# Five sets of edits in a four-layer cross-attention and RWKV kernel: the order of the first attention, its copies, and where the last norm and the channel mixes keep their data

## The chip, the cores and the metric

The kernel runs on one core of a Trainium2 chip, in one launch. The metric is the device time of that launch in microseconds (us). Three runs of the kernel before gave 2950.38, 2953.61 and 2958.53 us; the median, 2953.61 us, is the time that the change is held against.

The engines are named as in the profile: PE does matrix products and transposes, PEld loads its weights, DVE is the vector engine, ACT the scalar engine, POOL the general one (GpSimd), and SP issues the DMAs. Each engine works through its own instructions in order and waits on semaphores for what others produce.

## The reference, cut to what is computed

There are 8 sequences of 112 tokens and 512 channels (x), and for each a context of 375 rows of 512. Everything is float32. Four layers follow one another:

```python
# layer 0: one-head cross-attention of x on the context
q, k, v = x @ w_q.T, ctx @ w_k.T, ctx @ w_v.T
x = x + alpha * (softmax(q @ k.T / sqrt(512)) @ v) @ w_o.T
# layers 1 and 2: RWKV; the state comes from the first 18 rows of the context
xa = ln(x); sx = shift(xa) - xa                      # time mix
k, w, v, r, g = projections of xa + sx * (maa + lora(xa, sx))
s = k v^T + exp(-exp(w)) * s, token after token      # a scan over 112 tokens
x = x + (group_norm(r s) * silu(g)) @ Wo.T
xc = ln(x)                                           # channel mix
x = x + sigmoid(xr2 @ Wfr.T) * (relu(xk2 @ Wfk.T) ** 2 @ Wfv.T)
# layer 3: two cross-attentions of 16 heads of 128 on the context, then an MLP
x = x + attention(ln1(x), ctx);  x = x + attention(ln2(x), ctx)
x = x + gelu(ln_mlp(x) @ w_fc1 + b_fc1) @ w_fc2 + b_fc2
```

## The kernel before

**Layout.** Channels lie on the 128 partitions in four blocks (NC = 4), tokens along the free axis (896, in two halves of 448). x stays in SBUF from start to end. A pool `wpool` of four 8 KB slots (tag "w") holds the weights of all layers in turn. Each stage opens its own pools and closes them, and the next stage's pools take the same addresses: a pool that overlies a closed one can be used only once that one is free.

**Who orders the instructions.** The code is a Python program that emits instructions; a planner then orders each engine's instructions by their place in the program and by when it expects their inputs. Inside `tc.manual_schedule(engines=ORDERED)` PE, DVE, ACT and POOL keep the written order. In the kernel before only the scan of the time mixes does that (L682). The DMAs of SP are ordered by the planner everywhere.

**Layer 0** (L224 to L356). `w_qk` is formed as a product of the turned (transposed) w_q and w_k, q as its product with x, and `w_vo` from the turned w_v and w_o. Then the loop at L324 goes over the eight sequences: load the next context (four buffers, L232), turn the context into rows (L328, 12 transposes, three PSUM evictions by DVE), four score products (L336), softmax over DVE and ACT (L214 to L220), three transposes of the probabilities (L340), 12 products with the rows (L346), and a copy to z by ACT (L349). The last step, `ps_o`, multiplies z by w_vo; DVE adds it to x (L353). All of layer 0 is left to the planner.

For every second sequence `park` (L251) writes seven combinations of a pair of contexts to DRAM (`blocks`), which later layers read: six plain copies by DVE (L261), eight differences by POOL (L263), and five DMAs (14 for the first pair). It has one SBUF buffer, `blocks`, so a `park` begins when the DMAs of the one before have read it.

**Filling.** `values()` (L823) computes the values and part of the keys of layer 3 from the parked blocks (PE line L933). It is a generator; layers 1 and 2 call `fill(n)` at the places where PE would otherwise wait. It begins by loading weights (L842), four sums of them by POOL (L849 to L852), and a difference of two biases by DVE (L979), which SP then stores (L981).

**Layers 1 and 2.** `rwkv_layers` (L796) builds four constant matrices (`heads`, `same`, an identity; L803 to L816) and runs `rwkv` twice: `time_mix_inputs` (L378; its first steps load W_g, W_v, W_k and W_r and reorder the columns of W_g and W_v by ACT and DVE, L419 and L420), the scan, and `channel_mix` (L723). The channel mix keeps xc, sx, kk, rr, xk2 and xr2 in one pool; rr and kk are used until its last product, the other four only until `ps_fr`.

**The end of layer 2** (L788 to L794). While PE does the second half of `ps_fv`, the first half of layer 3's first norm is computed whole: mean, difference, squares, variance, root, reciprocal (L195), product (L196). `layer_norm_half` (L166) is the helper of all norms; `fills` says how many filler pieces go in at its three PE waits.

**Layer 3.** `attention(1)` (L1199) starts with scale and offset of that first half, the norm of the second half, `token_sums`, and then the first queries (`ps_k1q`, L1093). Beside it `first_keys` (L1239) is the filler: it loads a key weight, sums of it by POOL (L1067 to L1070), contexts and blocks (`cx`, `cs`, `cy`; L1221, L1226, L1228), and gives 28 pieces of four matmul records each (L1166). Its pools are opened in the order near, t3v (`cs`, `wsk`), t3k (`kt`, `cy`), t3, t3w.

Of the kernel before, what the change touches and what calls it, by code (L numbers as in the profile page):

```python
# [22 lines left out]
F32 = mybir.dt.float32  # L23
# [85 lines left out]
def tile_kernel(ctx: ExitStack, tc: tile.TileContext, d: dict, out: bass.AP):  # L109
# [26 lines left out]

    mean_c = const.tile([P, P], F32, name="mean_c")
# [28 lines left out]
    def layer_norm_half(ps, work, y, h, scale, offset, name, room=None, bank=None, fills=(2, 2, 4), small_tag="rstd"):  # L166
# [22 lines left out]
        nc.scalar.activation(sq, y, AF.Square)  # L189
        fill(fills[1])  # L190
        var = over_channels(sq, "var")
        fill(fills[2])
        rstd = small("rstd", "")
        nc.scalar.activation(rstd, var, AF.Sqrt, bias=eps)
        nc.vector.reciprocal(rstd, rstd)  # L195
        nc.vector.tensor_mul(y, y, rstd.unsqueeze(1).to_broadcast([P, NC, NH]))  # L196
        if scale is not None:
            scale_by_channel(y, y, scale, offset)
# [23 lines left out]


    def layer0():  # L224
# [3 lines left out]
        with (  # L228

            tc.tile_pool(name="a0s", bufs=2, space=PSUM) as ps2,  # L230
            tc.tile_pool(name="a0c", bufs=4) as near,
            tc.tile_pool(name="a0", bufs=1) as keep,  # L232
# [18 lines left out]
            def park(b, c1, c2):  # L251
# [7 lines left out]
                for k in range(2):  # L259
                    for y, z in ((b11, c11), (b21, c21), (b22, c22)):  # L260
                        nc.vector.tensor_copy(y[:, k], z[:, k])  # L261
                    for y, z, less in ((t0, c12, c11), (t1, c22, t0), (t2, c22, c12), (t3, c21, t1)):
                        nc.gpsimd.tensor_sub(y[:, k], z[:, k], less[:, k])  # L263
# [22 lines left out]
            def turned(w, name):  # L286

                t = keep.tile([P, NC, C], F32, tag="turned", bufs=3, name=f"t_{name}")
                for o in range(NC):
                    p = mm(ps, f"ps_t{name}_{o}")  # L290
                    for k in range(NC):
                        nc.tensor.transpose(p[:, k * P : (k + 1) * P], w[:, k, o * P : (o + 1) * P], ident)
                    (nc.vector.tensor_copy if o % 2 else nc.scalar.copy)(t[:, o, :], p)
                return t

            def product(a, b, name, pool, scale=1.0):

                y = pool.tile([P, NC, C], F32, tag=name, name=name)
# [9 lines left out]
            w_qk = product(turned(w_q, "q"), turned(w_k, "k"), "w_qk", keep, 1.0 / math.sqrt(C))  # L308
            q = keep.tile([P, NC, N], F32, name="q0")
            z = last.tile([P, NC, N], F32, name="z0")  # L310
            project(
                ps,
                w_qk,
                lambda k, h: halves(x[:, k, :], h),
                lambda o, h, p: nc.scalar.copy(halves(q[:, o, :], h), p),
                "q0",
            )
            w_vo = product(turned(w_v, "v"), w_o, "w_vo", last)
            for b in range(B):
                tok = slice(b * L, (b + 1) * L)  # L320
                if b + 1 < B:
                    context(b + 1)
                cx = cxs[b]
                if b % 2:  # L324
                    park(b, cxs.pop(b - 1), cxs.pop(b))
                rows = work.tile([CT, 3, C], F32, tag="rows", name=f"rows0_{b}")
                for t in range(3):
                    p = mm(ps, f"ps_r0_{b}_{t}")[:CT, :]  # L328
                    for k in range(NC):
                        nc.tensor.transpose(  # L330
                            p[:, k * P : (k + 1) * P], cx[:, k, t * CT : (t + 1) * CT], ident
                        )
                    nc.vector.tensor_copy(rows[:, t, :], p)
                sc = ps2.tile([L, S], F32, tag="sc", name=f"sc0_{b}")
                for k in range(NC):
                    nc.tensor.matmul(sc, q[:, k, tok], cx[:, k, :], start=k == 0, stop=k == NC - 1)  # L336
                prob = softmax(work, sc, S, f"0_{b}")
                pt = ps2.tile([CT, 3, L], F32, tag="pt", name=f"pt0_{b}")
                for t in range(3):
                    nc.tensor.transpose(pt[:, t, :], prob[:, t * CT : (t + 1) * CT], ident[:L, :L])  # L340
                pts = work.tile([CT, 3, L], F32, tag="pts", name=f"pts0_{b}")
                nc.vector.tensor_copy(pts, pt)
                av = ps2.tile([P, NC, L], F32, tag="av", name=f"av0_{b}")
                for o in range(NC):
                    for t in range(3):
                        nc.tensor.matmul(  # L346
                            av[:, o, :], rows[:, t, o * P : (o + 1) * P], pts[:, t, :], start=t == 0, stop=t == 2
                        )
                nc.scalar.copy(z[:, :, tok], av)  # L349
# [33 lines left out]
    def time_mix_inputs(n, pre, names, ones_t, first, k, v, r, g, decay, rows):  # L383
# [7 lines left out]
        with (  # L391
# [21 lines left out]
            ws = {f: weight(f"{pre}W{f}") for f in "gvkr"}  # L413
# [309 lines left out]
    def channel_mix(n, pre, names, first):  # L723
        nonlocal filler
        with (
            tc.tile_pool(name=f"c{n}", bufs=1) as one,
            tc.tile_pool(name=f"cw{n}", bufs=2) as work,
            tc.tile_pool(name=f"cp{n}", bufs=6, space=PSUM) as ps,
        ):
            f_k, f_r, f_v = (weight(pre + names[f]) for f in ("Fk", "Fr", "Fv"))  # L730
# [20 lines left out]
            kk = one.tile([P, NC, N], F32, name=f"kk{n}")  # L751
            rr = one.tile([P, NC, N], F32, name=f"rr{n}")
# [29 lines left out]
            else:  # L782
# [8 lines left out]
                layer_norm_half(ps, work, y, 0, None, None, "ln3_1", ([sq], None), None, (1, 1, 1))  # L791
# [4 lines left out]
    def rwkv_layers():  # L796
        with tc.tile_pool(name="rc", bufs=1) as one:
            ones_t = one.tile([P, P], F32, name="ones_t")
            mean_h = one.tile([P, P], F32, name="mean_h")
            less_mean_h = one.tile([P, P], F32, name="less_mean_h")  # L800
            center_h = less_mean_h, mean_h
            pick = one.tile([P, 4, 4 * HB], F32, name="pick")
            with tc.tile_pool(name="rs", bufs=1) as setup:  # L803
                heads = setup.tile([P, P + P + HS - 1], F32, name="heads")
                nc.sync.dma_start(heads, d["heads"])

                nc.vector.tensor_copy(ones_t.rearrange("p (q h r) -> p q h r", q=4, h=HB), turned(heads[:, :P]))
                same = setup.tile([P, P], F32, name="same")
                for q in range(4):
                    nc.sync.dma_start(same[32 * q : 32 * (q + 1)], turned_rows(d["heads"][:, :P], q))  # L810
                nc.scalar.mul(mean_h.rearrange("p (q h r) -> p q h r", q=4, h=HB), turned(same), 1.0 / HS)
                nc.vector.tensor_sub(less_mean_h, identity(setup, "rs"), mean_h)

                for r in range(4):
                    at = P + HS - 1 - 4 * r
                    nc.vector.tensor_copy(pick[:, r], heads[:, at : at + 16 * HB - 3 : 4])  # L816
            first = one.tile([P, 2, NC, B], F32, name="first")
            nc.sync.dma_start(first, d["first"])
            for n in (1, 2):
                rwkv(n, ones_t, center_h, pick, first)  # L820


    def values():  # L823
# [151 lines left out]
        for i in (1, 2):  # L975
# [3 lines left out]
            nc.vector.tensor_sub(over, over, bv)  # L979
# [219 lines left out]
    def attention(i, ident, h_in, work, kv, ps, ps2, keep, near, mlp_norm):  # L1199
# [61 lines left out]
        for h in range(2):  # L1261
            if i == 1 and not h:
                scale_by_channel(halves(h_in, 0), shared.pop("normed"), *scales)
            else:
                fill(2)
                layer_norm_half(ps, work, halves(h_in, h), h, *scales, f"ln3_{i}", room, ln_bank, (3, 3, 4))
# [276 lines left out]
```

## Time and profile before

| | us |
|---|---|
| median of the runs | 2953.61 |
| the profiled execution | 2960.41 |
| its span, first to last instruction | 2958.3 |
| around the span | 2.1 |
| PE busy | 2862.2 (97%) |
| DVE busy | 1603.7 (54%) |
| ACT busy | 1009.1 (34%) |
| POOL busy | 872.6 (29%) |
| mean granted clock of PE | 0.990 |

The page gives busy time per engine, a strip of 40 slices of the span, the chain of work that ended last, and the costliest groups of instructions. A matmul in float32 appears as two records. A row of the timeline reads: start, duration, engine, line, operation, output and inputs, count. A row of the waits reads: engine, output, line, then whom it waited for, the total in us, how often, the longest. A row of the chain of waits reads: start, duration, what held the end at that time. In a table of windows each engine has its busy time; PEclk is the granted clock as a share of full speed.

By stage, from the windows: layer 0 runs to 162.4 us, the first time mix's inputs to about 350, layer 1's channel mix ends near 780, layer 2's near 1425, and layer 3 takes the rest.

### The profile page before, as it was taken

Reading aid. Unit: us, or ns where it says so; the run is one execution under the profiler, and the core shown is the slowest. Engines: PE = TensorE matmul, PEld = TensorE weight load, DVE = VectorE, ACT = ScalarE, POOL = GpSimd, SP = SyncE. Lnnn points to the kernel's source line nnn. Section 1 sums busy time; section 2 is a strip of 40 time slices with the busy share of each in tenths; the row PEclk is TensorE's granted clock in tenths of the full one; section 3 lists DMA queues with packets and bytes.
Section 4 is the critical chain, followed back from the end, with each engine's and each line's share of the span. In section 5 each row is a group of like instructions: output and inputs, shape, how many; then the busy total and the mean of one; then the engine's idle time right before and its main releaser. Section 6 shows DMA issues by size and latency. Waiting matters only on the chain.

```text
span 2958.3 us, 29826 instructions
## 1 busy us (share of the span) xinstructions
PE 2862.2 (97%) x10130; PEld 1561.7 (53%) x10130; DVE 1603.7 (54%) x2350; ACT 1009.1 (34%) x2004; POOL 872.6 (29%) x700
## 2 busy tenths in 40 slices
PE   8989999999999999999899999999999999999999
PEld 4734443344444433356465656666565656656544
DVE  1564188856342788643455555545555554545455
ACT  2123466534243565532332323232331323323311
POOL 2332178744331687642411010100302010000030
PEclk9999999999999999999999999999999999999999
DMA  6521498943321989642344444334332433432110
GB/s 256 174 70 42 134 284 249 273 129 124 94 67 58 269 239 288 195 137 70 116 130 128 130 128 130 108 119 141 94 120 98 142 108 120 140 112 80 44 53 25
DMA packets 198743, 400.82 MB, mean 135 GB/s; under 512 B 33224, under 2 KB 119528, under 8 KB 191808
## 3 DMA queue, kind: packets, MB, share of 16 engines
q1 hardware_dynamic: 198592, 398.91, 43.3%
q8 instruction: 81, 1.33, 0.2%
q14 instruction: 70, 0.57, 0.1%
HBM read 321.06 MB, written 77.91 MB: 135 GB/s over the span
## 4 chain that ended last, share of the span: by engine, by line
PE 80%; DVE 7%; POOL 4%; DMA 3%; issue 3%; ACT 3%; SPq 0%; DVEq 0%; POOLq 0%; ACTq 0%
PE ps_vk L933 13%; PE ps_k1k L1166 10%; PE ps_k5k L1166 7%; PE av L1335 6%; PE sc L1322 5%; PE pt L1325 3%; PE ps_o L161 3%; PE ps_fk L161 2%; PE ps_k1q L1093 2%; PE ps_r L487 2%; PE ps_k L487 2%; PE ps_k7q L1093 2%; PE ps_fr L161 2%; PE ps_k5q L1093 2%; PE ps_k5o L1093 1%
## 5 line engine op out<-in xcount | busy, mean ns | idle before, releaser
L933 PE MATMUL ps_vk<-wv,cv 128*128 128x512 f32 x1296 | 583.7, 601 | 13.9 <-ACT k L1031 6.3
L933 PEld LDWEIGHTS ps_vk<-wv,cv 128*128 128x128 f32 x1296 | 244.0, 192 | 338.1 <-issue 287.9
L959 POOL TENSOR_TENSOR k<-k,k 128x512 f32<-128x512 f32 (+1 forms) x153 | 200.2, 1309 | 321.5 <-ACT k L958 264.3
L694 DVE TENSOR_TENSOR_SCAN st<-decay,kv 128x904 f32<-128x904 f32 x128 | 260.7, 2037 | 17.9 <-POOL rs L698 4.4
L698 POOL TENSOR_TENSOR rs<-st,r 128x896 f32<-128x896 f32 x128 | 247.0, 1929 | 53.3 <-DVE st L694 44.1
L218 ACT ACTIVATE prob<-sc,top 112x376 f32<-112x376 f32 (+1 forms) x264 | 151.8, 575 | 322.3 <-DVE top L215 194.8
L1322 PE MATMUL sc<-k,q 128*112 128x376 f32 x512 | 201.1, 485 | 0.7 <-ACT prob L218 0.7
L1335 PEld LDWEIGHTS av<-pts,v 125*128 125x128 f32 (+1 forms) x1536 | 185.0, 193 | 31.4 <-DVE pts L1331 16.6
L1315 POOL COPY k<-over_k 128x4 f32<-128x4 f32 x64 | 13.7, 223 | 605.0 <-PE sc L1322 577.0
L1335 PE MATMUL av<-pts,v 125*128 125x112 f32 (+1 forms) x1536 | 189.1, 277 | 2.1 <-DVE pts L1331 1.9
L1166 PE MATMUL ps_k1k<-cs,wsk 128*128 128x375 f32 x480 | 178.7, 481 | 1.5 <-ACT p1k L1169 1.5
L215 DVE TENSOR_REDUCE top<-sc 112x1 f32<-112x376 f32 (+1 forms) x264 | 143.3, 544 | 64.2 <-PE sc L1322 52.0
L690 DVE TENSOR_TENSOR kv<-vp,k 128x904 f32<-128x904 f32 x128 | 141.4, 1105 | 60.0 <-ACT vp L592 54.6
L958 ACT COPY k<-ps_vk 128x512 f32<-128x512 f32 (+1 forms) x153 | 89.1, 583 | 174.7 <-PE ps_vk L933 172.0
L1031 ACT COPY k<-ps_vk 128x512 f32<-128x512 f32 (+1 forms) x153 | 89.1, 582 | 163.2 <-PE ps_vk L933 156.0
L1325 PEld LDWEIGHTS pt<-ident_l,prob 112*125 112x125 f32 (+1 forms) x768 | 97.9, 177 | 73.2 <-DVE prob L220 44.2
L1325 PE MATMUL pt<-ident_l,prob 112*125 112x112 f32 (+1 forms) x768 | 121.4, 277 | 3.4 <-DVE prob L220 2.3
L220 DVE TENSOR_SCALAR prob<-prob,total 112x376 f32<-112x376 f32 (+1 forms) x264 | 119.7, 454 | 8.0
L1166 PEld LDWEIGHTS ps_k1k<-cs,wsk 128*128 128x128 f32 x480 | 89.7, 190 | 59.8 <-issue 2.1
L592 ACT COPY vp<-vj 128x896 f32<-128x896 f32 x124 | 112.8, 910 | 10.8 <-DMA vj<-rows 6.9
L1173 DVE TENSOR_TENSOR k<-ps_k5k,u2k 128x375 f32<-128x375 f32 x52 | 28.5, 548 | 159.2 <-PE ps_k5k L1166 158.2
L1342 DVE TENSOR_TENSOR ctxt<-av,bv 128x448 f32<-128x448 f32 x64 | 39.9, 624 | 127.3 <-PE av L1335 127.2
(389 smaller groups left out, 4820.6 us busy)
## 6 DMA issues: line engine op xcount, KB each, us to landing
vj<-rows SPq DMA_DIRECT2D x124, 448.0 KB
cv<-blocks SPq DMA_DIRECT2D x181, 251.5 KB
cs<-blocks SPq DMA_DIRECT2D x120, 375.0 KB
wvs<-k SPq DMA_DIRECT2D x128, 256.0 KB
v<-wvs SPq DMA_DIRECT2D x64, 512.0 KB
cx<-in_ctxT SPq DMA_DIRECT2D x38, 750.0 KB
v<-wvs SPq DMA_DIRECT2D x64, 252.0 KB
wvs<-k SPq DMA_DIRECT2D x64, 224.0 KB
```

Of the source, the lines that this page charges most:

```text
L161: nc.tensor.matmul(p, w[:, k, o * P : (o + 1) * P], rhs(k, h), start=k == 0, stop=k == NC - 1)
L215: nc.vector.tensor_reduce(top, scores, AX.X, ALU.max, negate=True)
L218: nc.scalar.activation(prob, scores, AF.Exp, bias=top, accum_out=total)
L694: nc.vector.tensor_tensor_scan(flat(st), flat(decay[:, c]), flat(kv), 0.0, ALU.mult, ALU.add)
L698: nc.gpsimd.tensor_mul(by_batch(rs), st[:, :, :L], by_batch(r[:, c, :]))
L933: nc.tensor.matmul(to, left, right, start=start and n == 0, stop=k == 1, skip_group_check=True)
L959: nc.gpsimd.tensor_add(y, z, y)
L1093: nc.tensor.matmul(to, lhsT, rhs, start=start and k == 0, stop=k == 1, skip_group_check=not start)
L1166: nc.tensor.matmul(y, lhsT, rhs, start=start and k == 0, stop=k == 1, skip_group_check=True)
L1322: nc.tensor.matmul(sc, q[:, o, tok], kt[:, o, :], start=True, stop=True)
L1325: nc.tensor.transpose(pt[t][:nt, o, :], prob[:, t0 : t0 + nt], ident[:L, :L])
L1335: nc.tensor.matmul(av[:, o, :], v[:nt, t, o * HD : (o + 1) * HD], pts[:nt, t, o, :], start=t == 0, stop=t == 2,)
```

## The change

- **Layer 0** is written in an explicit order, in a `manual_schedule`, from the turned weights to the last copy to z. Each turn of the loop does the turning and scores of sequence b+1 and, between them, the transposes of the probabilities of b; the softmax of b+1 is split in two, with the products of b behind it.
- Six context buffers in place of four; contexts 1 to 5 are loaded at once, 6 and 7 in the loop.
- `w_qk` and the turned w_v move into `wpool`.
- The six copies of `park` go from DVE to ACT; the bias difference of `values` goes from DVE to POOL.
- The constant matrices are built in layer 0 (`patterns`), their loads issued behind contexts 1 to 5.
- The RWKV weights are requested in the order k, g, r, v.
- The channel mix has two pools, `lower` and `upper`. In layer 2 xc, sx, xk2 and xr2 are in the lower one and kk and rr in the upper one; in layer 1 the reverse.
- The first half of layer 3's first norm stops after the root (`hold`). Its reciprocal and product are done inside the norm of the second half, and its scale and offset after that.

The core of the diff (the new `patterns` holds what L803 to L816 held):

```diff
-    def layer_norm_half(..., small_tag="rstd"):
+    def layer_norm_half(..., small_tag="rstd", hold=False, beside=iter(())):
         nc.scalar.activation(sq, y, AF.Square)
+        next(beside, None)
         fill(fills[1])
         var = over_channels(sq, "var")
+        next(beside, None)
         fill(fills[2])
-        rstd = small("rstd", "")
+        rstd = sq[:, 0] if hold else small("rstd", "")
         nc.scalar.activation(rstd, var, AF.Sqrt, bias=eps)
-        nc.vector.reciprocal(rstd, rstd)
-        nc.vector.tensor_mul(y, y, rstd...)
-        if scale is not None:
-            scale_by_channel(y, y, scale, offset)
+        def scaled():
+            nc.vector.reciprocal(rstd, rstd)
+            yield
+            nc.vector.tensor_mul(y, y, rstd...)
+            if scale is not None:
+                scale_by_channel(y, y, scale, offset)
+            yield
+        if hold:
+            return scaled()
+        for _ in scaled():
+            pass
...
-            tc.tile_pool(name="a0c", bufs=4) as near,
-            tc.tile_pool(name="a0", bufs=1) as keep,
+            tc.tile_pool(name="a0c", bufs=6) as near,
+            tc.tile_pool(name="a0", bufs=2) as keep,
...
                     for y, z in ((b11, c11), (b21, c21), (b22, c22)):
-                        nc.vector.tensor_copy(y[:, k], z[:, k])
+                        nc.scalar.copy(y[:, k], z[:, k])
...
+            for b in range(1, 6):
+                context(b)
+            made = patterns(keep, ident)
+            next(made)
+            def scores(b, between):
...
+                turn(0)
+                turn(1)
+                part(0)
+                part(1)
+                turn(2)
+                between()
+                part(2)
+                part(3)
+                return rows, sc
...
+            with tc.manual_schedule(engines=ORDERED):
+                w_qk = product(turned(w_q, "q"), turned(w_k, "k"), "w_qk", wpool, "w", 1.0 / math.sqrt(C))
+                project(ps, w_qk, ..., "q0")
+                w_vo = product(turned(w_v, "v", wpool, "w"), w_o, "w_vo", last, "w_vo")
+                next(made)
+                rows, sc = scores(0, lambda: None)
+                park(1, cxs[0], cxs[1])
+                prob = normalized(*exponentials(0, sc))
+                for b in range(B):
+                    if b in (1, 2):
+                        context(b + 5)
...
+                    left = rows
+                    if b + 1 < B:
+                        rows, sc = scores(b + 1, transposes)
+                        prob, total = exponentials(b + 1, sc)
+                    else:
+                        transposes()
+                    if b in (1, 3, 5):
+                        park(b + 2, cxs[b + 1], cxs[b + 2])
+                    if b + 1 < B:
+                        normalized(prob, total)
+                    av = ps2.tile([P, NC, L], F32, tag="av", name=f"av0_{b}")
...
+                    nc.scalar.copy(z[:, :, b * L : (b + 1) * L], av)
...
-            ws = {f: weight(f"{pre}W{f}") for f in "gvkr"}
+            ws = {f: weight(f"{pre}W{f}") for f in "kgrv"}
...
-            tc.tile_pool(name=f"c{n}", bufs=1) as one,
+            tc.tile_pool(name=f"c{n}", bufs=1) as lower,
+            tc.tile_pool(name=f"cc{n}", bufs=1) as upper,
...
+            one, late = (lower, upper) if n == 2 else (upper, lower)
-            kk = one.tile([P, NC, N], F32, name=f"kk{n}")
-            rr = one.tile([P, NC, N], F32, name=f"rr{n}")
+            kk = late.tile([P, NC, N], F32, name=f"kk{n}")
+            rr = late.tile([P, NC, N], F32, name=f"rr{n}")
...
-                layer_norm_half(ps, work, y, 0, None, None, "ln3_1", ([sq], None), None, (1, 1, 1))
+                shared["rest"] = layer_norm_half(
+                    ps, work, y, 0, None, None, "ln3_1", ([sq], None), None, (1, 1, 1), hold=True
+                )
...
-            nc.vector.tensor_sub(over, over, bv)
+            nc.gpsimd.tensor_sub(over, over, bv)
...
             if i == 1 and not h:
+                rest = shared.pop("rest")
+                continue
+            fill(2)
+            layer_norm_half(..., (3, 3, 4), beside=rest if i == 1 else iter(()))
+            if i == 1:
                 scale_by_channel(halves(h_in, 0), shared.pop("normed"), *scales)
-            else:
-                fill(2)
-                layer_norm_half(..., (3, 3, 4))
```

## The prediction

> **What bounds the kernel.** The busy times come first: PE works 2862.2 of 2958.3 us. Only its 96 idle us, and the time it runs at half clock, can be won, so I sort the idle time by stage (windows; the second number is PE's busy time):
>
> ```profile
> 0.00:70.00 70.00, 59.72 (x170) 31.40 (x171) 12.84 (x24) 16.21 (x25) 15.66 (x22) 0.96 0.74 271
> 70.00:130.00 60.00, 57.31 (x360) 44.40 (x360) 32.16 (x67) 9.95 (x25) 14.06 (x16) 0.99 0.45 159
> 130.00:162.40 32.40, 28.77 (x90) 15.23 (x89) 15.32 (x19) 1.12 (x3) 10.70 (x6) 0.95 0.51 151
> 162.40:300.00 137.60, 129.22 (x340) 57.23 (x339) 72.44 (x88) 44.69 (x65) 45.64 (x47) 0.93 0.17 53
> ...
> 780.00:920.00 140.00, 134.45 (x375) 59.21 (x376) 73.76 (x87) 51.03 (x74) 51.13 (x51) 0.98 0.26 82
> ...
> 1410.00:1467.10 57.10, 47.01 (x126) 24.68 (x125) 30.11 (x26) 20.25 (x33) 31.20 (x28) 0.91 0.46 150
> ```
>
> Layer 0 (to 162.4) is idle 16.6 us, the seam between layers 2 and 3 10.1 us in 57 and at clock 0.91. These two the change can reach. PE's waits name their causes:
>
> ```profile
> PE mean_ln L182 <- DVE t_h L180: 4.1, 1, 4.1
> PE ps_o L161 <- DVE x L353: 3.6, 1, 3.6
> PE ps_w_vo L302 <- ACT w_vo L305: 3.3, 1, 3.3
> ...
> PE av L346 <- DVE pts L342: 2.7, 1, 2.7
> PE ps_k5k L1166 <- DMA cy<-in_ctxT: 2.5, 1, 2.5
> ```
>
> The chain of waits says what stood behind them; first three places of layer 0, then the seam:
>
> ```profile
> 53.77 8.84 DMA w_L_xattn_Wv_None<-in_L_xattn_Wv
> ...
> 65.24 10.01 PE ps_w_vo L302 x16
> ...
> 94.31 6.88 DMA cx<-in_ctxT
> ...
> 145.33 5.58 DVE over L979 x2
> ```
>
> ```profile
> 1421.66 1.13 POOL x L773
> ...
> 1426.88 2.84 POOL x L773
> ...
> 1431.75 8.15 DMA cy<-in_ctxT
> ```
>
> So in-order ACT and DVE stand behind an instruction whose DMA is late, while PE's PSUM banks wait for them.
>
> **Layer 0, what goes.** (a) ACT waited for W_v's load and couldn't evict w_vo: 3.3 us idle, then 16 records in 10.01 us where the pitch before was 0.43, so 6.9: 3.1 more at half clock. (b) DVE stood at a park copy whose context was loading: 2.7. (c) DVE stood 5.58 us in two `over` differences that had waited for their loads and ran beside POOL's weight sums of 2.6 us each: 3.6 idle, then 24 records in 10.98 us where 0.376 a record gives 9.0: 2.0. Sum 14.7. Next late in (c) is DVE's sum of x for the next norm (L180, 2.73 us instead of 0.63 beside the same POOL sums); the product of z gives a bank every 3.0 us and there are two, so I charge 1 us at most here, below. `over` on POOL goes behind the sums: two small operations, under 1.26 each (a 128x512 sum), hidden by the 12 us between the sums' end (150.4) and ps_vk (162.4); SP's store of it waits no later than now.
>
> **Layer 0, what comes.** In the written order the turning of w_v stands alone: the four score records in it (1.3 us) no longer fill the gaps of its two banks. Cost 1.3. At the last sequence nothing covers transpose, pts copy (0.51) and semaphores: 0.8. The loop itself: per sequence 12 transposes 1.31 (0.109 each), 8 score records of 0.316 = 2.53, 3 transposes 0.36, 24 products 2.68: 6.9 us. Beside them DVE has rows 3 x 0.68, pts 0.51, max 0.55, reciprocal 0.15, product 0.41: 3.7. The softmax needs 2.2 us from the last score to the probabilities (0.2 + 0.55 + 0.1 + 0.76 + 0.2 + 0.41) and is next used after 2.7 of products and 2.6 of turning and scores: 3.1 spare. PE stays dense. Net 14.7 - 2.1 = **12.6 us**.
>
> Here a rule speaks against the change. The Trainium skill ("TensorE: Matmul & The Clock Gate", "Part 4: PE-mode transpose") says that transposes don't count as activity for the clock gate; its Part 1 puts the cold stretch at some 3.4 us. Three us of lone w_v transposes would then let w_vo start at half clock, near (a)'s row of 3.1 again, and layer 0 would win 9.5. The row: from 6.1 to 14.0 us PE did only transposes, and the next product, w_qk, ran at 0.43 us a record at once, at granted clock 1.00. I take the row.
>
> **Park on ACT.** No ACT copy of 128x375 within SBUF is in the trace. From PSUM it takes 0.47 us (L1169), 128x896 within SBUF takes 0.91 (L592); I take 0.53, near the first: 3.2 us a park, no gain in itself since DVE was not full (its 24 copies of 0.53 leave a slack engine). New is what queues behind: the copy to z and the next Exp, and behind Exp PE's transposes. ACT has 6.9 - 0.76 - 0.53 - 3.2 = 2.4 us left, plus the 3.1: a park may stall 5.5 us unseen. It stalls if the single buffer isn't read out. The first park's sums no longer wait for ACT (POOL starts at the contexts' landing, near 25 us), its copies come at w_vo's end near 70, and its DMAs take what they took before from the last sum (30.2) to the next copy (41.1): 11. So the buffer is free near 84, wanted at 85.6. Later parks: copies 3, sums 7.1, DMAs of the last blocks 4 to 6, near 13.5 us, wanted every 13.8. Cost 0, tight. Contexts 1 to 5 (3.75 MB) go out behind w_o and vecs, so nothing that PE needs first moves; heads and same go behind them, land near 35 at the 350 to 440 GB/s of the first stretches, and are wanted at 69. Contexts 6 and 7 are wanted 28 us after their issue at least, and took 6.9.
>
> **Entry of layer 1.** Its 8.4 idle us and clock 0.93 hang on the norm's chain over DVE, ACT and POOL, which waits for layer 0's last bank in both kernels; it moves forward whole. SP loses five constant loads in front of the RWKV weights (they arrive about 20 us before use: nothing). The reordering of W_g and W_v (4 x 1.05 ACT, 4 x 0.70 DVE) may land here instead of beside w_qk and w_vo: 0 if beside ps_o, 7 if all on the norm's chain. They ran at 46 and 63 us, beside products; ps_o leaves ACT nearly empty (1.1 us in 32), so I take 0.5. Together with DVE beside the weight sums: **-1** (range +4 to -7). The order k, g, r, v: each slot is free by 69 us, use is after 190: 0.
>
> **Layer 1's two pools.** The trace shows that one pool is released as a whole: POOL's memset (781.05), SP's maa loads (782.2) and DVE's xa (781.02) all begin at the last use of rr, 780.99. After the change maa's pool lies only over the four tiles done at 755, so the loads go early; but xa also waits for mean_ln, which began at 779.84, just as the last bank came free, and took 1.0. The idle us at 787, 799 and 804 sum to 1.25; I take **0.5**.
>
> **The seam.** From 1424.96 to 1467.11 PE has 84 key records x 0.316 = 26.5 us and 1.7 of small products: 13.9 lost in 42.15, through waits on `cs`, `cy` and mean_ln and the half clock after them. SP and POOL stood still until the last x (1429.72), since all of the channel mix was one pool. By the tile sizes near, t3v and t3k end 1 KB below the upper pool (111.7 against 112.7 thousand bytes a partition, counted from the base of the values pool), so `cs`, `cy` and the sums of the key weight need only the lower pool, free at the end of ps_fr (1398): 27 us early, beside ps_fv, where DMA and POOL are half idle. The reciprocal (2.94) and product (2.01) leave the place where DVE's rr and POOL's x stood behind them: the last x ends near 1426.9, not 1429.7. In the second half's norm they cost 1.25 (the reciprocal outlasts ACT's 1.70 us square) and 0.4, and the scale of half one 2.7. Mean near 1427.7, variance 1436, root, reciprocal, product 1443, scales 1448: queries near 1449, not 1467. The cover is 28 pieces x 1.26 = 35 us of keys for 24 us of chain; it holds. I leave 1.5 of the 13.9 for the variance waits: **12.4**.
>
> **Sum.** 12.6 - 1 + 0.5 + 12.4 = 24.5. The profiled run: 2960.41 - 24.5 = 2935.9. It stood 6.8 above the median, which I take as the base: 2953.61 - 24.5 = **2929**.
>
> **Rivals.**
> 1. The early release fails, because a planner's wait or the SP order keeps `cs` and `cy` behind x. Then the seam wins only the 2.8 of the earlier x and about 1.5 of cold clock: 12.6 - 0.5 + 4.3 = 16.4; 2937. For: SP is in order, and stood here before. Against: the pools fit.
> 2. More: layer 1's entry, freed of the DVE block, also closes half of its 8.4 idle and of the clock lost there (0.07 x 137.6 = 9.6), and the 1 charged above and the rest of 780 to 805 come too: 4.2 + 4.8 + 1 + 0.75 = 10.8 more, 2918. Against: its waits are within the norm's chain.
> 3. Slower: `park` blocks ACT in layer 0. The first pair before took 26.3 us from first copy (14.8) to the next tile's (41.14, after 17.0 of waiting for the DMAs). If every park does, the first stall exceeds its cover by 26.3 - 15.9 - 5.5 = 4.9, and two more by 12.5; with the half clock after three gaps (2 to 3 each) 38 us: 2967. It cancels the gain from about 21.8 us a park. Against: the later park from 82.72 was over by 101.32, at most 18.6 (loss 7).
> 4. No change: layer 0's loop loses what its stalls give back (park near 18.6, the rule's 3.1), and rival 1 holds: 24.5 - 8.1 - 7 - 3.1 = 6.3; 2947.
>
> **How the numbers follow.** Chances: forecast 0.50 (own range 2921 to 2937), rival 1 0.15, rival 2 0.11, rival 3 0.13, rival 4 0.11. A measurement tells 0.3% from no change, about 8.9 us (2944.7 to 2962.5). Faster is the first three, 0.76; same rival 4, 0.11; slower 0.13. The range 2912 to 2950 holds all but rival 3 and the tails of 4 and 2, about 0.2.
>
> **What would show it.** Right: no PE wait in layer 0 beyond the first load except under 1 us, ps_o's end near 149; `cs` and `cy` issued before 1400 (less the shift), no wait of mean_ln over 1 us, queries 24 us after the end of ps_fv instead of 42, PEclk 1.00 at the seam. Wrong: PE's transposes of probabilities waiting on ACT, or ACT's park copies on DMAs for over 5 us (rival 3); SP's `cs` still behind POOL's x (rival 1); w_vo at 0.85 a record (the rule). The forecast falls if the stage table shows under 8 us won in either place.

## The result, and the profile after

The changed kernel takes 2950.97 us (median of 14 runs, 2946.05 to 2955.67); the kernel before, on the same chips, 2958.11 (14 runs, 2950.38 to 2967.76). The ratio is 0.9972, 95% interval 0.9961 to 0.9983: 7 us faster between the medians, 8 by the ratio, where 24.5 were forecast. The profiled executions show more, 2946.32 (span 2944.3) against 2960.41 (span 2958.3). Why these two differences disagree is a finding of its own, below.

First the windows of the changed kernel, the same stretches as before (second number: PE's busy time; then PEld, DVE, ACT and POOL; then granted clock, DMA share, GB/s):

```profile
0.00:70.00 70.00, 62.54 (x186) 33.03 (x187) 6.56 (x17) 16.72 (x29) 7.78 (x14) 1.00 0.52 201
70.00:130.00 60.00, 58.06 (x379) 46.51 (x378) 31.32 (x59) 20.16 (x48) 22.19 (x24) 1.00 0.76 251
130.00:162.40 32.40, 31.83 (x80) 14.68 (x79) 15.88 (x18) 6.41 (x8) 13.80 (x9) 1.00 0.49 147
162.40:300.00 137.60, 128.64 (x346) 58.08 (x345) 67.35 (x80) 48.20 (x70) 44.27 (x44) 0.93 0.17 54
780.00:920.00 140.00, 133.50 (x371) 58.63 (x371) 67.89 (x82) 51.02 (x76) 47.39 (x47) 0.95 0.18 57
1410.00:1467.10 57.10, 49.09 (x141) 25.94 (x141) 31.58 (x25) 22.62 (x39) 28.68 (x25) 1.00 0.31 103
```

Layer 0 (now over at 150) is nearly full and at full clock. The seam is at full clock too, but PE is still idle for 8.0 us of this window. And 780 to 920, layer 2's entry, has got worse: 0.95 instead of 0.98. PE's waits, as line, whom it waits for, us in total, times, longest:

```profile
PE var_ln L184 <- DVE part_var_ln L182: 9.7, 7, 3.6
PE ps_vk L997 <- ACT k L1095: 8.2, 7, 1.4
PE ps_t L528 <- DVE xx L519: 6.3, 9, 2.1
...
PE ps_k1k L1230 <- ACT k L1233: 3.2, 2, 2.8
...
PE var_ln L184 <- DVE t_h L182: 1.9, 1, 1.9
...
PE mean_ln L184 <- DVE t_h L182: 1.7, 1, 1.7
PE av L424 <- DVE pts L409: 1.5, 1, 1.5
```

The waits for `w_vo`, for `over` (behind DVE's x) and for `cy` are gone. What heads the list now was there before too, at 8.3, 6.8 and 5.0 us for the first three rows. New or longer are the key evictions of ACT (2.8 us at the longest, 1.3 before) and one `av` wait of 1.5.

The rest is read from stretches between marks on PE's timeline (us; starts and ends of groups of records). "Order undone" is run e1 below.

```
stretch                              before  before again  after   order undone
w_vo, first to last record            20.3      20.7        13.9      13.9
end of w_vo to first ps_o             54.6      60.4        54.8      53.1
ps_o of layer 0                       32.7      33.7        27.1      27.1
end of layer 0, on the clock         162.5     169.7       150.2     148.7
end of layer 0 to layer 1's ps_t      19.8      19.8        20.6      20.6
end of layer 1's ps_fv to ps_t        20.5      20.5        23.9      20.5
layer 2's ps_t to its ps_v            52.5      54.0        55.8      52.5
end of layer 2's ps_fv to queries     42.0      39.0        36.1      37.8
```

Between the two profiled executions of before and after, layer 0 wins 12.3 us and the seam 5.9; layer 1's entry gives back 0.8, layer 2's entry 3.4 up to `ps_t` and 3.3 after it. The remaining 3.4 of the 14.1 are spread over stretches that the change does not touch.

### The profile page after: what moved, and what is told of

It reads as the page before. It is cut to its first block, busy times and chain, and to the rows that moved or that the text cites. A ratio compares the mean times of both kernels' runs of the same rounds, so it can differ in the third digit from the quotient of the medians.

```text
span 2944.3 us, 29821 instructions
## 1 busy us (share of the span) xinstructions
PE 2858.2 (97%) x10130; PEld 1560.8 (53%) x10130; DVE 1591.8 (54%) x2324; ACT 1018.7 (35%) x2028; POOL 874.6 (30%) x700
## 4 chain that ended last, share of the span: by engine, by line
PE 81%; DVE 7%; POOL 3%; ACT 3%; DMA 3%; issue 2%; SPq 0%; DVEq 0%; POOLq 0%; ACTq 0%
PE ps_vk L997 13%; PE ps_k1k L1230 10%; PE ps_k5k L1230 7%; PE av L1412 6%; PE sc L1399 5%; PE ps_o L163 3%; PE pt L1402 3%; PE ps_fk L163 2%; PE ps_k1q L1157 2%; PE ps_k L565 2%; PE ps_r L565 2%; PE ps_k5q L1157 2%; PE ps_fr L163 2%; PE ps_k7q L1157 2%; PE ps_k5o L1157 1%
## 5 line engine op out<-in xcount | busy, mean ns | idle before, releaser
L231 ACT ACTIVATE prob<-sc,top 112x376 f32<-112x376 f32 x256 | 147.2, 575 | 295.9 <-DVE top L228 168.4
L1392 POOL COPY k<-over_k 128x4 f32<-128x4 f32 x64 | 13.8, 224 | 648.0 <-PE sc L1399 576.0
L1412 PEld LDWEIGHTS av<-pts,v 125*128 125x128 f32 (+1 forms) x1536 | 185.8, 193 | 31.3 <-DVE pts L1408 16.1
L228 DVE TENSOR_REDUCE top<-sc 112x1 f32<-112x376 f32 x256 | 139.0, 544 | 56.9 <-PE sc L1399 51.9
L233 DVE TENSOR_SCALAR prob<-prob,total 112x376 f32<-112x376 f32 x256 | 115.5, 452 | 7.7
```

The source lines that it names most:

```text
L231: nc.scalar.activation(prob, scores, AF.Exp, bias=top, accum_out=total)
L1412: nc.tensor.matmul(av[:, o, :], v[:nt, t, o * HD : (o + 1) * HD], pts[:nt, t, o, :], start=t == 0, stop=t == 2,)
```

## Experiments

Times are medians; the ratio is to the kernel before, with its 95% interval.

**The order of the RWKV weights.** The trace of the changed kernel at layer 2's entry (start, duration, engine, line; in brackets how long the engine had been idle, and for whom):

```profile
765.50 0.35 SPq L127 DMA_DIRECT2D w_L_xattn_Wv_None<-in_L_xattn_Wv  x1
767.31 2.02 DVE L189 TENSOR_TENSOR xa<-x,mean_ln 128x1792 f32<-128x1792 f32 x1 [1.11 <-PE mean_ln L184]
768.17 0.58 ACT L1095 COPY k<-ps_vk 128x512 f32<-128x512 f32 x1 [26.18 <-PE ps_vk L997]
770.50 1.99 ACT L497 COPY turnv<-w_L_xattn_Wv_None 128x1024 f32<-128x1024 f32 x2 [1.74 <-DMA w_L_xattn_Wv_None<-in_L_xattn_Wv]
772.40 0.58 ACT L1095 COPY k<-ps_vk 128x512 f32<-128x512 f32 x1
772.87 1.70 ACT L191 ACTIVATE sq_ln<-xa 128x1792 f32<-128x1792 f32 x1
773.03 3.19 PE L997 MATMUL ps_vk<-wv,cv 128*128 128x512 f32 x6 [1.31 <-ACT k L1095]
```

Loaded last, W_v gets its slot only as `ps_fv` ends, so its load goes out at 765.50. ACT reaches the copies that reorder it, stands idle 1.74 us for the load, then copies for 1.99 (both halves together; the expectation below takes them for 1.99 each). Behind them in ACT's queue wait the eviction for which PE stands (1.31) and the square of the norm: its input is there at 769.33, it starts at 772.87, 3.5 us late. Three runs put the order back, wholly or in part:

```diff
-            ws = {f: weight(f"{pre}W{f}") for f in "kgrv"}
+            ws = {f: weight(f"{pre}W{f}") for f in "gvkr"}                            # e1
+            ws = {f: weight(f"{pre}W{f}") for f in ("kgrv" if n == 1 else "gvkr")}    # e2
+            ws = {f: weight(f"{pre}W{f}") for f in "kgvr"}                            # e5
```

> The changed kernel with the RWKV weights loaded in the old order g, v, k, r in both layers, nothing else. Theory A (the order made W_v the last weight to arrive at layer 2's entry, at 770.5 us; its two ACT copies of 1.99 us each stand in front of the eviction of k and of the first square, and hold up the norm): the first ps_t of layer 2 comes some 3 us earlier than 789.4 and ps_v of layer 2 some 5 us earlier than 845.2, granted clock of 780 to 920 back from 0.95 to 0.98; in layer 1 the W_v copies return to the evictions of w_vo, which costs 1 to 3 us there (w_vo 13.75 us for its 32 records becomes 15 to 17). Sum 1 to 4 us faster than the changed kernel, median 2947 to 2950. Theory B (the loss at layer 2's entry is in the norm's own chain and in the early loads of the mixing weights, whatever the order): marks of layer 2 unchanged within 1 us, time 0 to 3 us slower than the changed kernel through w_vo.

> The changed kernel with the order g, v, k, r in layer 2 only; layer 1 keeps k, g, r, v. Theory A: layer 2's entry as in the run with the old order in both layers (ps_t 3 us, ps_v 5 us earlier than 789.4 and 845.2), layer 0 and 1 as in the changed kernel: 3 to 6 us faster than it, median 2945 to 2948. Theory B: no change, within 1 us of it.

> The changed kernel with only the last two weights exchanged: k, g, v, r instead of k, g, r, v; W_v is no longer the last to arrive and its two ACT copies go ahead of the eviction of k in layer 2 with its load already done. Theory A (what costs is that the weight that needs reordering is loaded last): the stretch from the end of layer 1's ps_fv to the first ps_v of layer 2 is back from 79.7 us to 73.0, as with the order g, v, k, r; time 5 to 8 us under the changed kernel (2943 to 2946). Theory B (what costs is k in the first slot, or g and v in later slots): the stretch stays within 1.5 us of 79.7 and the time within 2 us of the changed kernel.

Measured: e1 2940.25 us, 0.9944 (0.9923 to 0.9964), faster than either theory said; e2 2943.24, 0.9949 (0.9929 to 0.997); e5 2943.32, 0.995 (0.9934 to 0.9966). The same place in e1:

```profile
765.64 0.35 SPq L127 DMA_DIRECT2D w_L_xattn_Wr_None<-in_L_xattn_Wr  x1
767.46 2.02 DVE L189 TENSOR_TENSOR xa<-x,mean_ln 128x1792 f32<-128x1792 f32 x1 [1.11 <-PE mean_ln L184]
768.32 0.58 ACT L1095 COPY k<-ps_vk 128x512 f32<-128x512 f32 x1 [26.18 <-PE ps_vk L997]
769.59 1.70 ACT L191 ACTIVATE sq_ln<-xa 128x1792 f32<-128x1792 f32 x1 [0.69 <-DVE xa L189]
```

The late load is now W_r, which needs no copy, and the square starts 0.11 us after its input. From the end of `ps_fv` to `ps_t` the stretch is 20.5 to 20.6 us in every run where W_v isn't last (e1, e2 and e5 to e11) and 23.9 to 24.2 where it is (after, e3, e4). That is 3.4 us, and the exchange of the last two letters alone brings them back. The 3.3 us after `ps_t` I had counted with them wrongly: that stretch takes 52.5 to 55.8 us under either order.

The order costs a second time, where I did not expect it. In layer 0's loop the old order put the W_v copies beside `w_vo`; the new one puts them into the sequences. The changed kernel, first SP's issue of the load, then ACT, DVE and PE:

```profile
92.27 1.26 SPq L127 DMA_DIRECT2D w_L_xattn_Wv_None<-in_L_xattn_Wv  x1
...
100.23 2.54 ACT L292 COPY blocks<-cx 128x375 f32<-128x375 f32 x6 [0.88 <-DMA blocks<-blocks]
102.67 0.52 ACT L427 COPY z<-av 128x448 f32<-128x448 f32 x1
103.09 1.99 ACT L497 COPY turnv<-w_L_xattn_Wv_None 128x1024 f32<-128x1024 f32 x2
104.17 1.07 DVE L498 COPY w_L_xattn_Wv_None<-turnv 128x1024 f32<-128x1024 f32 x1 [1.66 <-ACT turnv L497]
105.16 0.68 DVE L356 COPY rows<-ps_r 125x512 f32<-125x512 f32 x1
...
106.40 2.90 PE L424 MATMUL av<-pts,rows 125*128 125x112 f32 x24 [1.49 <-DVE pts L409]
```

The slot of the fourth weight was free when `w_vo` ended, at 68.4 us, but its load went out only at 92.27, behind the DMAs of `park` in SP's queue. So W_v's copies fall among the sequences. A park whose buffer was still being read out holds them up (0.88 us); DVE, in its own order, stands 1.66 us for ACT's half of the copy, and `rows` and `pts`, for which PE waits, come behind it: 1.49 us here, and 3.28 in e2, whose layer 0 is the same program:

```profile
101.98 2.53 ACT L292 COPY blocks<-cx 128x375 f32<-128x375 f32 x6 [2.53 <-DMA blocks<-blocks]
...
104.84 1.99 ACT L497 COPY turnv<-w_L_xattn_Wv_None 128x1024 f32<-128x1024 f32 x2
105.92 1.20 DVE L498 COPY w_L_xattn_Wv_None<-turnv 128x1024 f32<-128x1024 f32 x1 [3.31 <-ACT turnv L497]
...
108.28 4.53 PE L424 MATMUL av<-pts,rows 125*128 125x112 f32 x24 [3.28 <-DVE pts L409]
```

In e1 the same park waits too, and PE does not:

```profile
100.17 2.54 ACT L292 COPY blocks<-cx 128x375 f32<-128x375 f32 x6 [0.66 <-DMA blocks<-blocks]
...
104.90 2.83 PE L424 MATMUL av<-pts,rows 125*128 125x112 f32 x24
```

The 24 products behind the longer wait take 4.53 instead of 2.90 us. This wait for `pts` is 1.5, 3.3, 2.5 and 2.4 us in the four runs with W_v last in layer 1 (after, e2, e3, e4), and absent in the five with the old order and park on ACT. With `k, g, r, v` in layer 1 the stretch from `w_vo` to `ps_o` takes 54.8, 58.2, 57.4 and 57.3 us (after, e2, e3, e4), with the old order 53.0 to 53.3 with the same park on ACT (e1, e6, e7, e9, e10): 3.8 in the mean. e5 lies at 53.5, its W_v loaded third, at 68.56, and copied four sequences earlier. The feared cost in `w_vo`'s evictions did not appear: 13.9 us for the 32 records in both.

**The seam.** One pool for each channel mix, and the last norm of the first half in one piece:

```diff
-            one, late = (lower, upper) if n == 2 else (upper, lower)
+            one, late = lower, lower                                  # e3
```
```diff
-                shared["rest"] = layer_norm_half(..., (1, 1, 1), hold=True)
+                layer_norm_half(..., (1, 1, 1))                        # e4, e6 (e6: with "gvkr")
...
-                rest = shared.pop("rest")
+                scale_by_channel(halves(h_in, 0), shared.pop("normed"), *scales)
```

> The changed kernel with each channel mix in one pool again (xk, xr, xc, sx, kk and rr together), all else as changed. Theory A (two pools let cs, cy and the weight sums go at 1390 instead of 1420, and that is what won the seam's 5.8 us): the first queries of layer 3 come 4 to 6 us later than 1453.6 less what layer 2's entry shifts, granted clock of 1410 to 1467 back near 0.91 from 1.00; layer 2's entry loses 0 to 1 us. Sum 4 to 7 us slower than the changed kernel. Theory B (the seam's gain is from the scale of half 0 and the reciprocal having moved, the early loads were hidden anyway): seam within 1 us of the changed kernel.

> The changed kernel with the last norm of the first half not split: reciprocal, product and scale of half 0 in one piece as before, two pools and all else as changed. Theory A (the split does little as the reciprocal of 2.94 us and the product of 2.33 us run at 1416.8 and 1420.1 before the last x in both): the queries within 1.5 us of 1453.6, time within 1.5 us of the changed kernel. Theory B (the split takes the scale of half 0, 2.7 us on ACT, and part of DVE out of the chain): queries 3 to 6 us later, time 3 to 6 us slower.

> The changed kernel with the order g, v, k, r and the last norm in one piece. Theory A (the split works against the seam once the two pools are there, since the scale of half 0 then stands on ACT between key evictions at a later place): end of layer 2's ps_fv to the first queries 34 to 35.5 us instead of the 37.8 of the run with the old order, and 2 to 4 us under that run's 2940. Theory B (the 34.6 seen once without the split is chance): 36 to 38 us, time within 1.5 us of 2940.

Measured: e3 2951.4, 0.9973 (0.9963 to 0.9983); e4 2947.07, 0.9965 (0.9949 to 0.9981); e6 2938.27, 0.9931 (0.9915 to 0.9948). The times of e3 and of the changed kernel can't be told apart, so what one pool costs is read from the traces. From the end of `ps_fv` to the queries, with the 84 key records that stand there in every run:

```
                                             us            PE idle       granted clock
one pool, no split: before, again, e9        42.0 39.0 38.8  8.8 6.2 6.0  0.88 0.87 0.87
one pool, split: e3                          39.1          7.4           0.91
two pools, split: after, e8                  36.1 36.1     6.8 6.8       1.00 1.00
two pools, split: e1, e2, e5, e11            37.8          6.8           0.95
two pools, no split: e4, e6                  34.6 34.6     4.5 4.5       1.00 1.00
two pools, split, DVE written: e7, e10       35.3 36.5     5.7 5.3       1.00 0.95
```

Two pools bring some us, mostly by the clock: with the split 36.1 to 37.8 against 39.1, without it 34.6 against 38.8. The split takes part of them away, 1.5 to 3.2 us: PE stands idle 6.8 us with it and 4.5 without. Neither expectation of e4 allowed for a split that costs. PE's waits in the stretch of e6:

```profile
PE ps_k1k L1228 <- ACT k L1231: 1.7, 1, 1.7
...
PE ps_k1k L1228 <- ACT u2k L1231: 1.0, 1, 1.0
PE mean_ln L184 <- DVE t_h L182: 0.6, 1, 0.6
```

The key waits for ACT are 1.7 us at the longest, where the changed kernel has 2.8 (its key evictions stand behind four scales of half 1, 2.71 us), and the mean's wait is 0.6 instead of 1.7. Why the split made the planner choose the worse order isn't settled. What the two pools did, and what the split did not, is plain in the changed kernel's trace:

```profile
1390.48 1.97 SPq L1290 DMA_DIRECT2D cs<-blocks  x4
...
1415.10 1.26 POOL L1131 TENSOR_TENSOR wsk<-w_L_xattn_wk 128x512 f32<-128x512 f32 x1
...
1416.77 2.94 DVE L201 RECIPROCAL sq_ln<-sq_ln 128x448 f32<-128x448 f32 x1
...
1419.28 1.27 POOL L1134 TENSOR_TENSOR wsk<-w_L_xattn_wk,wsk 128x512 f32<-128x512 f32 x1
1419.63 0.56 DVE L853 TENSOR_TENSOR rr<-ps_fv,rr 128x448 f32<-128x448 f32 x1
...
1420.11 2.33 DVE L203 TENSOR_TENSOR y_ln<-y_ln,sq_ln 128x1792 f32<-128x1792 f32 x1
1420.51 2.92 POOL L854 TENSOR_TENSOR x<-x,rr 128x448 f32<-128x448 f32 x1
```

`cs` goes out 27 us before the end of `ps_fv`. But the reciprocal and the product of half 0 still stand before and beside the last x, as before the change, and four weight sums now stand ahead of it on POOL. e7 writes DVE's order out, so that they come after:

```diff
-                for _ in filler:
-                    pass
+                with tc.manual_schedule(engines={mybir.EngineType.DVE}):
+                    for _ in filler:
+                        pass
...
+            with tc.manual_schedule(engines={mybir.EngineType.DVE}):      # i == 1
             fill(2)
             layer_norm_half(..., beside=rest)
```

> The changed kernel with the order g, v, k, r, and with DVE's order at the seam written out, so that the product rr of the last piece and the mean's sums stand ahead of the reciprocal and the product of half 0, as the prediction took for granted. Theory A (the seam fell short of the forecast because the planner left reciprocal and product ahead of the last x): the last x ends 2 to 3 us sooner after the end of ps_fv than 5.9 us, the wait of mean_ln goes, and queries come 32 to 35 us after the end of ps_fv instead of 37.8; time 2936 to 2938. Theory B (POOL's four weight sums, 5.4 us, hold the last x anyway, and PE has its 86 records of keys to do whatever the norm does): queries 36 to 38 us after, time within 1.5 us of 2940.

Measured: 2937.66 us, 0.9939 (0.9921 to 0.9957); queries after 35.3 us, 2.5 fewer than e1. In e7:

```profile
1411.95 0.62 DVE L853 TENSOR_TENSOR rr<-ps_fv,rr 128x448 f32<-128x448 f32 x1 [0.67 <-PE ps_fv L163]
1412.37 1.26 POOL L1133 TENSOR_TENSOR wsk<-wsk,w_L_xattn_wk 128x512 f32<-128x512 f32 x1
1413.72 1.27 POOL L1135 TENSOR_TENSOR wsk<-w_L_xattn_wk,wsk 128x512 f32<-128x512 f32 x1
1414.94 1.13 POOL L854 TENSOR_TENSOR x<-x,rr 128x448 f32<-128x448 f32 x1
...
1416.87 0.99 PE L184 MATMUL mean_ln<-t_h,mean_c 128*128 128x448 f32 x2 [2.43 <-DVE t_h L182]
```

Both theories hold a part. DVE gives rr at 0.66 us after `ps_fv`, not 2.7, and x takes 1.13 us instead of 2.92 once no DVE product runs beside it. But x waits 2.4 us for the weight sums, and PE as long for the mean.

**What remains of the change without the seam**, and what its parts in layer 0 are worth:

```diff
# e9: "gvkr", one pool, norm in one piece        # e11: "gvkr", planner's order in layer 0
-            with tc.manual_schedule(engines=ORDERED):
+            with ExitStack():
# e8: "gvkr", and in park
-                        nc.scalar.copy(y[:, k], z[:, k])
+                        nc.vector.tensor_copy(y[:, k], z[:, k])
# e10: e7, and
-            nc.gpsimd.tensor_sub(over, over, bv)
+            nc.vector.tensor_sub(over, over, bv)
```

> The changed kernel with the order g, v, k, r, each channel mix in one pool and the last norm in one piece: of the change only the first attention and the move of the over differences to POOL are left. Theory A (the parts add up): layer 0 ends near 148.7 us as in the other runs with that order, 13.8 ahead of before; layer 1's entry gives back 0.8; layer 2's entry takes 73.0 us as before; the end of layer 2's ps_fv to the queries takes 42 us as before, so that the seam wins nothing. Time 12 to 14 us under before, 2944 to 2946. Theory B (the seam's gain comes from layer 0's earlier end or from other shifts and not from the pools): 36 to 38 us at the seam, time near 2940.

> The changed kernel with the order g, v, k, r and the 24 block copies of the first attention back on DVE, in the written order. Theory A (ACT is the better place: a park copy that waits on the DMAs of the single buffer then stands on DVE in front of the row copies that free PE's banks, and takes 3 us of DVE a sequence pair): the stretch from the end of w_vo to the first ps_o is 3 to 8 us longer than the 53.1 of the run with park on ACT, time 2943 to 2948. Theory B (the buffer's turnaround sets the pace wherever the copies stand): within 1 us of 53.1 and of 2940.

> The run with the written order of DVE at the seam, with the two over differences back on DVE. Theory A (they hold DVE up among the additions of ps_o, as the prediction charged 5.6 us to them): the stretch of ps_o grows from 27.1 to 31 to 33 us; layer 1's entry may win back 0.8; time 3 to 5 us over 2937.7. Theory B (with the contexts loaded ahead their loads are there in time, and they cost DVE under 0.5 us): ps_o stays at 27 to 28 us and the time within 1.5 us.

> The changed kernel with the order g, v, k, r, and with the first attention left to the planner: loads ahead, pools and engines as changed, without the written order. Theory A (the written order is needed, since the planner puts park copies of ACT in front of evictions of w_vo, at a place where the single block buffer is still being read out): w_vo takes 5 to 12 us more than 13.9, and layer 0 ends 8 to 15 us after 148.7; time 2948 to 2955. Theory B (the loads ahead alone bring the gain): layer 0 ends within 2 us of 148.7, time within 2 us of 2940.

e9: 2946.53, 0.9954 (0.9935 to 0.9973). Layer 0 ends at 148.7 as expected; the seam takes 38.8, not the 42 I had expected (nor does the kernel before take 42 again, below). e8: 2943.12, 0.9955 (0.9938 to 0.9971): from `w_vo` to `ps_o` 57.3 us instead of 53.1, with one PE wait of 2.5 for `rows`, which stood behind DVE's block copies; so ACT is the better place. e10: 2946.27, 0.9966 (0.9955 to 0.9978), 8.6 over e7; layer 0 explains 5.9 of it, and layer 1's entry gives back 0.8 as expected; the other 3.5 stay open. Its DVE and its PE:

```profile
137.91 5.12 DVE L1044 TENSOR_TENSOR over<-over,bv 4x512 f32<-4x512 f32 x2 [2.80 <-DMA maa<-in_L_xattn_maa_w]
...
143.68 10.98 PE L163 MATMUL ps_o<-z,w_vo 128*128 128x448 f32 x24 [3.93 <-DVE x L431]
```

That is the stall of the kernel before, to the half-clock tail of 10.98 us. e11: 2944.36, 0.996 (0.9944 to 0.9975), its layer 0 over at 149.2, 0.5 us after e1's. I had expected 8 to 15: the written order as such is worth next to nothing there, once the contexts are loaded ahead. Its time is 4 us above e1's, with intervals that overlap, and layer 0 does not explain it.

> The kernel before once more, for the spread of its stage marks. If the marks are repeatable, the end of layer 0 lies within 0.5 us of 162.5, layer 2's entry within 0.5 us of 73.0 and the seam within 1 us of 42.0; the profiled time anywhere in the runs' 2948 to 2968. If layer 0 wanders by 3 us or more, as the changed kernel's does, the gain of layer 0 is known to that much only.

The profiled run took 2962.8. Layer 2's entry to `ps_t` repeats to 0.01 us, but layer 0 ends at 169.7 instead of 162.5 and the seam takes 39.0 instead of 42.0. The wait that was 2.7 us in the first trace (`av` for `pts`, behind a park copy) is twice as long:

```profile
PE av L346 <- DVE pts L342: 5.4, 1, 5.4
PE ps_w_vo L302 <- ACT w_vo L305: 3.9, 1, 3.9
PE ps_o L161 <- DVE x L353: 3.6, 1, 3.6
```

So waits for DMAs and the clock after them wander from one execution to the next, by 7.2 us in layer 0 of the kernel before. What the change wins there is known to no more than that.

## Why the prediction was wrong

**Layer 0: right in mechanism; the size is known to some 7 us.** 12.6 was forecast. Between the first pair of profiles 12.3 was measured, against the second profile of the kernel before it is 19.5; that 12.3 lies so near is in part luck. (a) `w_vo` fell by 6.4, as summed. The rule of the Trainium skill weighed there, that transposes don't count as activity for the clock gate, was to have `w_vo` start at half clock; it ran its 32 records in 13.9 us, 0.43 each, straight after the turning of w_v. That alone is no test, since the turning took only 2.7 us (51.7 to 54.5), less than the cold stretch of 3.4 that the prediction names. What speaks against the rule is the prediction's own row: from 6.1 to 14.0 us nothing but transposes, and then `w_qk` at full clock. (c) `ps_o` fell by 5.6, as summed, and e10 shows `over` as its cause. (b) went too, but W_v's copies put a wait of the same kind in its place; without them layer 0 wins 13.9 (e1). "Park on ACT: cost 0, tight" holds: ACT did wait 0.4 to 2.5 us for the buffer, and PE lost nothing by it in e1, at waits of 0.7 and 1.3, nor in e7, at 1.4 and 2.5. The sum behind it was too small, though: 3, 7.1 and 4 to 6 make 14.1 to 16.1, not 13.5, and e1's parks follow each other after 14.4 and 14.3 us where 13.8 were put. Rival 3 had the right place and overrated the price: its stall needed the copies of W_v behind it to reach PE.

**The step that failed: "The order k, g, r, v: each slot is free by 69 us, use is after 190: 0."** In layer 1 the slot was free at 68.4, as put, and the product came after 190; but the load waited in SP's queue until 92.27, and the first use of W_v is not its product but the ACT copy that reorders it. In layer 2 the slot comes free only as `ps_fv` ends, and the copy stands in ACT's in-order queue ahead of the norm. Measured, where 0 was put: 3.4 us there, 3.8 in the mean in layer 0's loop (1.7 in the changed kernel's own profile); the medians of after and e1 differ by 10.7. I had placed layer 1's copies "beside ps_o" for 0.5 us and asked nothing about layer 2's.

**The seam: right on the release, mis-sized.** `cs` and `cy` went out at 1390 as forecast, and the half clock is gone. Of 12.4 the profiles show 5.9. The term that was mis-sized is the idle time left over: the sum left 1.5 us of the 13.9, and PE stood idle for 6.8 (8.8 before). Nor could the queries come 24 us after `ps_fv`: the 28.2 us of keys and small products counted in the same paragraph stand ahead of them in every run. Two things lie behind the shortfall. The sum took for granted that "reciprocal and product leave the place": the planner left them there, and put POOL's weight sums ahead of the last x as well. And 42.0 was a high draw of the base: with one pool the stretch took 42.0, 39.0, 39.1 and 38.8, so that against their mean two pools with the split (36.1 to 37.8) win some 2.5 us, without it or with DVE's order written out some 3 to 5. Why PE's idle time is longer with the split is argued from the waits shown above, and stays open in part.

**Layer 1's entry** gave back 0.8 where 1 was charged, and e10 shows `over` on POOL as its cause. **Layer 1's two pools**: 0 where 0.5 was put; with the old order the stretch is 20.5 us in one pool (e9) and in two.

**Rivals.** Rival 1 did not happen: SP issued early. Rival 2's closing of layer 1's entry did not either. The gain is near the 6.3 us of rival 4, but not for its reasons: neither the rule nor a late `cs` was at work, and the park reached PE only through W_v's copies.

Taken together: 24.5, less 7.2 for the order, less 6.5 in the seam, leaves 10.8, between the 7 or 8 of the runs and the 14 of the profiles; 2951 lies 1 us beyond the range. This is an estimate put together from several runs, and the wandering of layer 0 and of the seam is as large as its terms. With the weights in the old order and DVE's order written out (e7) the profiled run takes 2936.28, 24.1 under the first profile of before, and the medians differ by 20. e6 and e7 beat both kernels and can't be told apart.

**Why profile and runs disagree.** The forecast stood on one execution and a median of three runs, 2953.61; 14 runs put before at 2958.11. The profile of the changed kernel, 2946.32, is the second lowest of its 14 runs, and that of the kernel before, 2960.41, lies above its median: so the two profiles show a difference of 14 where the medians show 7. Late in the kernel, in a stretch that the change leaves alone, after and e1 show PE nearly as busy over the same 105 us, under another granted clock. First after, then e1:

```profile
2675.00:2780.00 105.00, 98.65 (x357) 58.72 (x356) 56.99 (x94) 35.44 (x68) 10.47 (x8) 0.93 0.16 53
```
```profile
2675.00:2780.00 105.00, 97.58 (x367) 56.64 (x366) 59.41 (x96) 38.55 (x73) 10.45 (x8) 1.00 0.15 50
```

From the first `ps_o` there to the end of the last norm after takes 94.0 us and e1 88.4: 5.6 us that belong to neither change. One and the same program differs there too: before has a granted clock of 0.95, before again 1.00. One pair of profiles can be off by as much as this change is worth.

## What to carry to other kernels

For a load that is moved, ask who touches the tile first: where that is a reordering copy in an in-order queue, the tile belongs early, and the last slot belongs to the tile that only a product reads. Check the question in every layer that runs the same code, not only in the one whose times are at hand. Splitting an operation does not move it: where a planner sets the order, look in the trace for where the piece went, or write the order out.

## What the hardware showed unexpectedly

Two things. A POOL sum of 128x448 takes 1.13 us where no long DVE product runs beside it (e7) and 2.92 beside one of 128x1792 (after), so an engine off the path stretched the step that was on it. And the granted clock over a stretch with nearly the same waits came out at 0.92 to 1.00 between executions (2675 to 2780 us: before 0.95, before again 1.00, after 0.93, e1 1.00, e10 0.92); between after and e1 that made 5.6 us.
